# The first pair of each diffusion step: attention groups and scalings put ahead of the looks, and fewer GpSimd operations, in a two-layer graph kernel

## The chip, the cores and the metric

The kernel runs on one core of one Trainium2 chip. The metric is the device time of one execution in microseconds; lower is better. Differences are read in per cent of some 3760 us. The engines are called by the profile's names: PE (TensorE), ACT (ScalarE), DVE (VectorE), POOL (GpSimd), and SP (SyncE), which here only issues DMAs. "PEq", "DVEq" and "SPq" are the engines' instruction queues.

## The reference, cut to what matters

A graph of n = 2708 nodes with 512 features goes through two layers. Layer 0 is graph attention with 8 heads. Layer 1, which the change concerns, is a diffusion in two steps; it has a dense S (the adjacency plus the identity) and an attention that keeps, in each row, the smallest set of largest probabilities whose sum reaches 0.9:

```python
Rf = S / S.sum(axis=1, keepdims=True)
Rb = S / S.sum(axis=0)[:, None]
Xf, Xb, Xa = X, X, X
Z = 0
for s in range(2):
    Q, K = Xa @ W1, Xa @ W3
    logits = Q @ W2 @ K.T
    vals, idx = sorted(logits, descending)          # in each row
    k_i = sum(cumsum(softmax(vals)) < 0.9) + 1
    A = softmax(logits where rank < k_i else -inf)
    Xf, Xb, Xa = Rf @ Xf, Rb @ Xb, A @ Xa
    Z = Z + (Xf @ U1[s] + Xb @ U2[s] + Xa @ U3[s])
Y = X + Z                                           # then layer norm, and the residual
```

The sorted and cumulated part is not done by sorting: the kernel looks for a threshold in each row above which the mass is 0.9.

## The kernel before, in words

**Tiling.** The 2708 rows are 22 tiles of 128 rows (the last has 20). Two tiles are a pair (`grp`, 11 pairs), four tiles a quad. Layer 0 takes until about 1086 us of the profiled span, step 0 of layer 1 until about 2311, step 1 the rest. In layer 1 `S` and the split features lie in HBM and are streamed for each quad; the values `va` and the keys stay in SBUF.

**What is done for a pair**, in `class Logits` (L490) and the functions behind it:

- `queries` (L499) loads the queries `q_t`. `products` (L508) multiplies them with the keys on PE (L517), six chunks for a tile, and ACT copies each chunk from PSUM into the logits tile `p` (L519). The pool of `p` has four buffers, so the products of pair g+2 can be copied only when the search of pair g is done with its tiles. Its end is a branch on DVE (L884).
- `exp` (L522) takes the row maxima on DVE (L544) and returns a list of steps: for each tile `root` (L552 and L549: the exponentials of half the logits, for their sum) and `full` (L556: the exponentials in place, with their sum) on ACT; `points` (L559 to L572: three first guesses of the threshold, small operations on POOL); the looks (L549), two passes of ACT over `p` for each of three points and two tiles, twelve in all; and `masses` (L574 to L577, POOL), which makes of the looks' sums the mass above each guess.
- `search` (L592) runs on DVE: it picks the bracket from the looks (L619 to L641), then makes rounds (two in step 0, four in step 1), each with a pass over `p` for each tile (L624). After its first round it calls `early`, which starts `exp` of the next pair. Then it calls `late` (below) and `finish` (L793). `finish` makes a copy of `p` below the threshold in `keep` (L800), takes its eight largest (L802; in step 1 twice), finds the exact cut, and writes the kept row into `keep` (L722, or L728 where step 1 ranks ties). A switch at L884 goes to rarely used arms: ties (L736), more rounds (MORE_ROUNDS), bisection. `rden` (L901) is the reciprocal of the kept mass.
- `attended` (L996): the kept rows are turned on PE (L1006) in groups of four tiles, copied to `at` by ACT (L1010), and multiplied with `va` (L1025). There are 6 groups for a row tile, 12 for a pair. The scaled sum is `xa` (L1033).
- `part` (L941): the diffusion of a quad, S times the features. One `product` (L949) loads `hl` (L955) and `s_r` (L957) on SP's queue and makes 8 matmuls (L961). At the end of a part its `scaled` steps (L964) scale the rows on ACT (L967) into the tile `xe` of a pool with two buffers, store that on POOL's queue to `xfb_d` (L968), and in step 0 split it for the next step (`split_rows`, L175: L181 and L182 on DVE, a store on POOL's queue at L183, two buffers).
- `diffused` (L986) loads the scaled rows of a pair back as `x0`, `x1` (L991, SP). `mixed` (L1040) turns them and `xa` on PE (L147) and multiplies them with the three `U` (L1056 loads, L1058).

**The order of the work.** On PE, ACT, DVE and SP the program's order is the order of execution (`manual_schedule`); POOL's order is the planner's. Each pass of the main loop (index g, L1165 on) overlaps three pairs: the logits of pair g+2, the search of pair g+1 and the attention of pair g. Work is put between the matmuls of attention from two lists: `fills` (the steps of `exp`, mostly for ACT) and `others` (products, scalings, loads of the diffusion); `paced(list, n)` runs the next n of a list. The lists `looks` and `left` exist only for the first pairs: the pass g = -1 has no attention, so it leaves six looks and the masses, and the scalings of the part that it worked on (eight in step 0, four in step 1), to the pass g = 0. Before the change that pass puts lg[2]'s products first, then all left looks, then search and attention, with the left scalings and the loads of `diffused` at the head of `others`.

Of the kernel before, what the change touches and what calls it, by code (L numbers as in the profile page):

```python
# [9 lines left out]
F32 = mybir.dt.float32  # L10
# [5 lines left out]
OP = mybir.AluOpType  # L16
# [8 lines left out]
P = 128  # L25
# [6 lines left out]
X_LO = math.exp(-4.0)  # L32
# [5 lines left out]
ABOUT = (0.88, 1.0, 1.12)  # L38
# [15 lines left out]
def kernel(  # L54
# [415 lines left out]
    for s in range(STEPS):  # L470
        for i in range(2):
            nc.vector.memset(powers[:, s, i], GUESS[s][i])
    weights = const.tile([P, G + 1], F32, name="weights")
# [14 lines left out]
    class Logits:  # L488
# [33 lines left out]
        def exp(self, looks=True):  # L522
# [5 lines left out]
            self.tot = small.tile([P, G], F32, name="tot")  # L528
            self.half = small.tile([P, G], F32, name="half")
# [8 lines left out]
            if self.ragged:  # L538
                for x in (self.tot, self.half, self.above, self.signs, self.pts):
                    nc.gpsimd.memset(x, 1.0)  # L540
# [18 lines left out]
            def points():  # L559
                x0 = small.tile([P, 2, G], F32, name="x0")  # L560
                gp.tensor_tensor(x0[:, 0], self.tot, powers[:, self.s, 0], op=OP.pow)
                gp.tensor_tensor(x0[:, 1], self.half, powers[:, self.s, 1], op=OP.pow)
                gp.tensor_tensor(x0[:, 0], x0[:, 0], x0[:, 1], op=OP.mult)
                gp.tensor_scalar(x0[:, 0], x0[:, 0], math.exp(GUESS[self.s][2]), X_LO * 1.5, op0=OP.mult, op1=OP.max)
                for j, m in enumerate(ABOUT):
                    gp.tensor_scalar(self.pts[:, j, 0], x0[:, 0], m, 0.9995, op0=OP.mult, op1=OP.min)
                gp.tensor_tensor(self.th, self.pts[:, :, 0], self.pts[:, :, 0], op=OP.mult)
                gp.tensor_tensor(self.th, self.th, self.th, op=OP.mult)
                gp.tensor_scalar(self.nth, self.th, -1.0, None, op0=OP.mult)  # L569
                gp.tensor_scalar(self.thr, self.tot, P_NUC, None, op0=OP.mult)  # L570
                gp.tensor_scalar(self.top, self.tot, 1.0 + CURVE, None, op0=OP.mult)
                gp.tensor_scalar(self.cap, self.tot, CAP, None, op0=OP.mult)  # L572
# [10 lines left out]
            if looks:  # L583
                for i, t in enumerate(self.grp):
# [8 lines left out]
    def search(lg, looked, early, late):  # L593
# [199 lines left out]
        def finish(go):  # L793


            for i, pr in tiles:
                t, m = th[:pr, i:i + 1], kept[:pr, 1, i:i + 1]
                for e in range(0, nx, 8):
                    vs, ss = vn[:pr, i, e:e + 8], sn[:pr, i, e:e + 8]
                    v.scalar_tensor_tensor(keep[i][:pr], ps_[i][:pr], t, ps_[i][:pr], op0=OP.is_lt, op1=OP.mult,  # L800
                                           accum_out=left[:pr, i:i + 1] if e else None)
                    v.max(vs, keep[i][:pr])  # L802
# [105 lines left out]
    for s in range(STEPS):  # L908
        last = s == STEPS - 1
        with ExitStack() as st:  # L910
# [26 lines left out]
            def part(half, b):  # L937
# [26 lines left out]
                def scaled(t, ps, i, inv, to):  # L964
                    pr = rows[t]
                    x = work.tile([P, D], F32, name="xe")
# [14 lines left out]
            def paced(steps, n):  # L981
                for step in steps[:n]:
                    step()
                del steps[:n]
# [10 lines left out]
            def attended(grp, keep, rden, fills, others, then):  # L995
# [21 lines left out]
                for n, (i, t, cs) in enumerate(steps):  # L1017
# [18 lines left out]
                    at = nxt  # L1036
                return xa, at

# [107 lines left out]
            with tc.manual_schedule(engines={PE, ACT, DVE, SP}):  # L1146
# [18 lines left out]
                for g in range(-1, NP):  # L1165

                    fills = []
                    if g + 2 < NP:
                        lg[g + 2].products()
                    paced(looks, len(looks))  # L1170
# [7 lines left out]
                    if g >= 0:  # L1178
                        left.append(lambda g=g: rows_in.extend(diffused(pairs[g])))
                    others = left + part(half, g + 2)  # L1180
                    left = []
# [6 lines left out]
                    def late(g=g):  # L1188
                        if g >= 0:
                            keep, rden = ready  # L1190
                            if g:
                                paced(others, 1)
                            final = g == NP - 1 and not last
                            xa, v_t = attended(pairs[g], keep, rden, fills, others,
                                               lambda: None if final else turned_rows(pairs[g], rows_in[0]))
# [53 lines left out]
```

## Time and profile before

| | |
|---|---|
| median of three runs | 3761.26 us (3754.86, 3761.26, 3762.85) |
| the profiled execution | 3750.71 us |
| its span on the core | 3748.9 us |
| mean granted TensorE clock | 0.959 |
| layer 0; step 0; step 1 (from the timeline) | to 1086; to 2311; to 3749 us |

The profiled execution is one of its own, beside the three runs; the span is the part of it from the first to the last instruction. The tables of the profile are for that one execution.

A timeline line reads: start in us, duration in us, engine, line of the kernel, operation, output and inputs with sizes, how many instructions are taken together, and in brackets the idle time of the engine just ahead, with what ended it. A line of waits reads: engine and what it wanted to run, the releaser, total us, times, and the longest. The clock in stretches says how fast PE was allowed to run:

```
stretch of the span        PEclk
1196 to 1327 us (pair 0, step 0)   0.86
1430 to 2311 us (rest of step 0)   0.98
2490 to 2633 us (pair 0, step 1)   0.88
2633 to 3640 us (rest of step 1)   0.99
```

### The profile page before, as it was taken

The numbers are of one execution on the slowest core, as the hardware profiler recorded it, in microseconds if no ns is written. First come the engines' busy times: TensorE is split into PE (matmuls) and PEld (weight loads), VectorE is DVE, ScalarE is ACT, GpSimd is POOL, SyncE is SP. The second block draws the span as 40 slices with busy tenths as digits, with TensorE's granted clock in tenths as the row PEclk, the third lists the DMA queues.
The fourth block names the chain that finished last, engine by engine and source line by source line (L and its number), as shares of the span: only waits on it lengthen the run. The fifth ranks groups of instructions, "written<-read, shape, count | busy, mean of one in ns | idle before, by whom it ended". The sixth has DMA issues, their size and how long they took to land. (4 is left out here: it accounts for less than half of the span.)

```text
span 3748.9 us, 35397 instructions
## 1 busy us (share of the span) xinstructions
PE 3377.5 (90%) x11143; PEld 1759.3 (47%) x11143; DVE 2612.2 (70%) x4814; ACT 1540.2 (41%) x2334; POOL 836.7 (22%) x1187
## 2 busy tenths in 40 slices
PE   8999999999855898989899899668999999999888
PEld 4433333333433455545455453435555665556442
DVE  4588898989946536474454652966879788777991
ACT  2344202111026565555666622334644556445511
POOL 4115151423331121121212120302222111111101
PEclk9999999999977899999999999889999999999999
DMA  3476424233144555454545353836556765567552
GB/s 116 155 258 224 155 80 136 89 101 109 50 147 163 190 185 178 154 178 147 196 148 207 108 189 119 300 101 234 194 192 210 252 207 188 192 210 240 191 200 72
DMA packets 276459, 634.09 MB, mean 169 GB/s; under 512 B 37209, under 2 KB 70441, under 8 KB 273243
## 3 DMA queue, kind: packets, MB, share of 16 engines
q1 hardware_dynamic: 249183, 540.99, 43.4%
q0 software_dynamic: 27024, 90.30, 6.4%
q8 instruction: 89, 1.46, 0.2%
q14 instruction: 163, 1.34, 0.1%
HBM read 509.07 MB, written 122.10 MB: 168 GB/s over the span
## 5 line engine op out<-in xcount | busy, mean ns | idle before, releaser
L1025 PE MATMUL a<-va,at 128*128 128x512 f32 (+2 forms) x1936 | 898.0, 603 | 57.9 <-ACT at L1010 57.7
L961 PE MATMUL q<-hl,s_r 128*128 128x512 f32 x2904 | 823.3, 430 | 69.1 <-DMA s_r<-s_d 67.6
L429 PE MATMUL po<-e,fw 128*65 128x512 f32 (+4 forms) x2112 | 836.7, 551 | 31.1 <-DVE e L427 22.6
L427 DVE SCALAR_TENSOR_TENSOR e<-r_b,kk,a_c 128x512 f32<-128x512 f32 (+4 forms) x1056 | 750.9, 740 | 64.9 <-PE po L429 13.8
L961 PEld LDWEIGHTS q<-hl,s_r 128*128 128x128 f32 x2904 | 547.9, 191 | 313.5 <-issue 158.9
L549 ACT ACTIVATE junk_a<-p,nth 128x2708 uint8<-128x2708 f32 (+1 forms) x240 | 613.1, 2554 | 93.4 <-POOL nth L569 89.8
L1025 PEld LDWEIGHTS a<-va,at 128*128 128x128 f32 (+2 forms) x1936 | 339.9, 188 | 428.5 <-issue 347.2
L429 PEld LDWEIGHTS po<-e,fw 128*65 128x65 f32 (+1 forms) x2112 | 285.3, 139 | 542.9 <-issue 267.4
L1058 PE MATMUL a<-u_k,v_t 128*128 128x512 f32 (+1 forms) x1056 | 490.2, 601 | 22.0 <-ACT xa L1033 14.7
L624 DVE SCALAR_TENSOR_TENSOR junk<-p,th 128x2708 bf16<-128x2708 f32 (+1 forms) x132 | 402.3, 3048 | 4.0
L1010 ACT COPY at<-t 128x512 f32<-128x512 f32 (+3 forms) x308 | 140.2, 476 | 440.3 <-PE t L1006 439.7
L1058 PEld LDWEIGHTS a<-u_k,v_t 128*128 128x128 f32 (+1 forms) x1056 | 188.8, 186 | 240.0 <-issue 185.6
L517 PE MATMUL t<-keys,q_t 128*128 128x452 f32 x528 | 167.8, 445 | 108.6 <-ACT p L519 87.9
L800 DVE SCALAR_TENSOR_TENSOR keep<-p,th 128x2708 f32<-128x2708 f32 (+1 forms) x44 | 133.4, 3033 | 132.2 <-PE t L1006 131.0
L181 DVE TENSOR_SCALAR split_hl<-xe 128x512 int32<-128x512 int32 (+1 forms) x44 | 19.0, 433 | 272.9 <-ACT xe L967 232.5
L802 DVE MAX8 vn<-keep 128x8 f32<-128x2708 f32 (+1 forms) x66 | 196.8, 2982 | 2.3
L519 ACT COPY p<-t 128x452 f32<-128x452 f32 (+2 forms) x264 | 132.3, 539 | 147.4 <-DVEq L884 74.8
L411 ACT ACTIVATE s_c<-a_c 128x512 fp32r<-128x512 f32 (+3 forms) x132 | 76.2, 578 | 247.1 <-DMA a_c<-in_adj_t_dram 121.8
L517 PEld LDWEIGHTS t<-keys,q_t 128*128 128x128 f32 x528 | 92.0, 211 | 179.9 <-ACT p L519 141.4
L1006 PE MATMUL t<-ident,keep 128*128 128x128 f32 (+1 forms) x968 | 147.4, 274 | 24.4 <-DVE keep L752 16.7
L1006 PEld LDWEIGHTS t<-ident,keep 128*128 128x128 f32 (+1 forms) x968 | 115.1, 139 | 107.6 <-issue 80.4
L544 DVE TENSOR_REDUCE nmx<-p 128x1 f32<-128x2708 f32 (+1 forms) x44 | 129.2, 2967 | 36.1 <-ACT p L519 35.8
(294 smaller groups left out, 3099.1 us busy)
## 6 DMA issues: line engine op xcount, KB each, us to landing
s_r<-s_d SPq DMA_DIRECT2D x330, 256.0 KB
hl<-vhl_d SPq DMA_DIRECT2D x132, 512.0 KB
u_k<-in_L_gnn_U_dram SPq DMA_DIRECT2D x264, 256.0 KB
hl<-fhl_d SPq DMA_DIRECT2D x132, 512.0 KB
hl<-bhl_d SPq DMA_DIRECT2D x132, 512.0 KB
arow<-in_adj_dram SPq DMA_DIRECT2D x21, 1354.0 KB
s_d<-s_c SPq DMA_DIRECT2D x88, 256.0 KB
a_c<-in_adj_t_dram SPq DMA_DIRECT2D x84, 256.0 KB
```

The source lines that it names most:

```text
L427: nc.vector.scalar_tensor_tensor(e[:pr, :cw], r_b[:pr, i, :cw], kk[:pr, t, hd:hd + 1], a_c[t][:pr, :cw], op0=OP.max, op1=OP.mult)
L429: nc.tensor.matmul(po[i][:, :cw], lhsT=fw[:pr, t, hd, :], rhs=e[:pr, :cw], start=(t == 0), stop=(t == NT - 1))
L517: nc.tensor.matmul(pl[:, :c1 - c0], lhsT=q[:, i], rhs=self.keys[:, c0:c1], start=(i == 0), stop=(i == 1))
L549: nc.scalar.activation(junk[:pr], self.p[i][:pr], func, **kw)
L624: v.scalar_tensor_tensor(junk_b[:pr], ps_[i][:pr], th, ps_[i][:pr], op0=OP.is_ge, op1=OP.mult, accum_out=dst)
L800: v.scalar_tensor_tensor(keep[i][:pr], ps_[i][:pr], t, ps_[i][:pr], op0=OP.is_lt, op1=OP.mult, accum_out=left[:pr, i:i + 1] if e else None)
L802: v.max(vs, keep[i][:pr])
L961: nc.tensor.matmul(half[j], lhsT=s_r[:, j * P:(j + 1) * P], rhs=hl[:, h], start=(c == 0 and h == 0), stop=(c == NT - 1 and h == 1))
L1006: nc.tensor.transpose(pt[:rows[c], j, :pr], keep[i][:pr, cols[c]], ident[:pr, :pr])
L1010: nc.scalar.copy(at[:r, j0:j1, :pr], pt[:r, j0:j1, :pr])
L1025: nc.tensor.matmul(pa[:pr], lhsT=at[:rows[c], j, :pr], rhs=va[:rows[c], c, :], start=(c == 0), stop=(c == NT - 1))
L1058: nc.tensor.matmul(pz[i][:rows[t]], lhsT=v_t[i][:, k, :rows[t]], rhs=u_k, start=(n == 0 and k == 0), stop=(n == 2 and k == KD - 1))
```

## The change

Eight edits, all in layer 1:

1. In the first pass with attention (g = 0) the left scalings go ahead. In step 1 all four come ahead of lg[2]'s products; in step 0 four come ahead of them and four behind them, ahead of attention. Before, they were paced between the attention groups.
2. In step 1, four products of the next part go ahead of lg[2]'s products in that pass.
3. `attended` becomes a generator that stops after each group, and in that pass it is advanced one group for every two of the left looks. Before, all left looks came ahead of attention.
4. The loads of `diffused` go, in that pass, behind the first third of `others`; in the other passes they go to its head, as before.
5. `points` makes 10 GpSimd operations for 13: one power over the two sums, one product with the three factors, one clamp. The factors are a constant tile, filled once by six DVE memsets.
6. An empty step stands between `points` and the looks, so each look comes one place later in `fills`.
7. `finish` writes the passes below the threshold of both tiles into keep[0].
8. `xe` has four buffers in step 0; in step 1, for the first two parts, the odd tiles use a tile `xw` with two buffers of its own.

The number of instructions is the same on PE, ACT and SP; on DVE there are six more. The diff, cut to its core:

```diff
--- before.py
+++ after.py
@@ -470,6 +470,10 @@
     for s in range(STEPS):
         for i in range(2):
             nc.vector.memset(powers[:, s, i], GUESS[s][i])
+    about = const.tile([P, STEPS, len(ABOUT), G], F32, name="about")
+    for s in range(STEPS):
+        for j, m in enumerate(ABOUT):
+            nc.vector.memset(about[:, s, j], m * math.exp(GUESS[s][2]))
     weights = const.tile([P, G + 1], F32, name="weights")
     for i in range(G + 1):
         nc.vector.memset(weights[:, i:i + 1], float(1 << i))
@@ -525,8 +529,8 @@
             _, small, _ = self.pools
             gp = nc.gpsimd
             grp = self.grp
-            self.tot = small.tile([P, G], F32, name="tot")
-            self.half = small.tile([P, G], F32, name="half")
+            self.sums = small.tile([P, 2, G], F32, name="sums")
+            self.tot, self.half = self.sums[:, 0], self.sums[:, 1]
             self.pts = small.tile([P, NA, 3, G], F32, name="pts")
             self.th = small.tile([P, NA, G], F32, name="th_a")
@@ -536,7 +540,7 @@
             self.signs = small.tile([P, NA, G], F32, name="signs", bufs=1)
             self.ragged = any(rows[t] < P for t in grp) or len(grp) < G
             if self.ragged:
-                for x in (self.tot, self.half, self.above, self.signs, self.pts):
+                for x in (self.sums, self.above, self.signs, self.pts):
                     nc.gpsimd.memset(x, 1.0)
             nmx = small.tile([P, 2, G], F32, name="nmx1")
             for i, t in enumerate(self.grp):
@@ -558,13 +562,12 @@
             def points():
                 x0 = small.tile([P, 2, G], F32, name="x0")
-                gp.tensor_tensor(x0[:, 0], self.tot, powers[:, self.s, 0], op=OP.pow)
-                gp.tensor_tensor(x0[:, 1], self.half, powers[:, self.s, 1], op=OP.pow)
+                gp.tensor_tensor(x0, self.sums, powers[:, self.s], op=OP.pow)
                 gp.tensor_tensor(x0[:, 0], x0[:, 0], x0[:, 1], op=OP.mult)
-                gp.tensor_scalar(x0[:, 0], x0[:, 0], math.exp(GUESS[self.s][2]), X_LO * 1.5, op0=OP.mult, op1=OP.max)
-                for j, m in enumerate(ABOUT):
-                    gp.tensor_scalar(self.pts[:, j, 0], x0[:, 0], m, 0.9995, op0=OP.mult, op1=OP.min)
-                gp.tensor_tensor(self.th, self.pts[:, :, 0], self.pts[:, :, 0], op=OP.mult)
+                x = self.pts[:, :, 0]
+                gp.tensor_tensor(x, x0[:, 0].unsqueeze(1).to_broadcast([P, NA, G]), about[:, self.s], op=OP.mult)
+                gp.tensor_scalar(x, x, X_LO * 1.2, 0.9995, op0=OP.max, op1=OP.min)
+                gp.tensor_tensor(self.th, x, x, op=OP.mult)
                 gp.tensor_tensor(self.th, self.th, self.th, op=OP.mult)
                 gp.tensor_scalar(self.nth, self.th, -1.0, None, op0=OP.mult)
                 gp.tensor_scalar(self.thr, self.tot, P_NUC, None, op0=OP.mult)
@@ -581,6 +584,8 @@
                 steps += [lambda a=(i, rows[t]): root(*a), lambda a=(i, rows[t]): full(*a)]
             steps.append(points)
             if looks:
+                steps.append(lambda: None)
                 for i, t in enumerate(self.grp):
                     for j in range(NA):
                         for func, to in ((AF.Relu, self.above), (AF.Sign, self.signs)):
@@ -793,13 +798,14 @@
         def finish(go):
             for i, pr in tiles:
                 t, m = th[:pr, i:i + 1], kept[:pr, 1, i:i + 1]
                 for e in range(0, nx, 8):
                     vs, ss = vn[:pr, i, e:e + 8], sn[:pr, i, e:e + 8]
-                    v.scalar_tensor_tensor(keep[i][:pr], ps_[i][:pr], t, ps_[i][:pr], op0=OP.is_lt, op1=OP.mult,
+                    v.scalar_tensor_tensor(keep[0][:pr], ps_[i][:pr], t, ps_[i][:pr], op0=OP.is_lt, op1=OP.mult,
                                            accum_out=left[:pr, i:i + 1] if e else None)
-                    v.max(vs, keep[i][:pr])
+                    v.max(vs, keep[0][:pr])
                     if e:
                         m = left[:pr, i:i + 1]
                         v.tensor_tensor(m, tot[:pr, i:i + 1], m, op=OP.subtract)
@@ -963,7 +969,11 @@
                 def scaled(t, ps, i, inv, to):
                     pr = rows[t]
-                    x = work.tile([P, D], F32, name="xe")
+                    if last and b < 2 and t % 2:
+                        x = work.tile([P, D], F32, name="xw", bufs=2)
+                    else:
+                        x = work.tile([P, D], F32, name="xe", bufs=2 if last else 4)
                     nc.scalar.activation(x[:pr], ps[:pr], AF.Copy, scale=inv[:pr, t:t + 1])
                     nc.gpsimd.dma_start(out=xfb_d[i, cols[t], :], in_=x[:pr])
                     if not last:
@@ -1034,7 +1044,15 @@
                         if not last:
                             nc.gpsimd.dma_start(out=xa_d[cols[t], :], in_=xa[i][:pr])
                     at = nxt
+                    yield
                 return xa, at
+            def rest_of(work_):
+                while True:
+                    try:
+                        next(work_)
+                    except StopIteration as done_:
+                        return done_.value
             def turned_rows(grp, v):
                 return [transposed(up, ps_t, v[i], rows[t], "v_t") for i, t in enumerate(grp)]
@@ -1165,9 +1183,15 @@
                 for g in range(-1, NP):
                     fills = []
+                    held = len(left)
+                    paced(left, held if last else held // 2)
+                    others = left + part(half, g + 2)
+                    left = []
+                    if g == 0 and last:
+                        paced(others, 4)
                     if g + 2 < NP:
                         lg[g + 2].products()
-                    paced(looks, len(looks))
                     if g + 3 < NP:
                         lg.append(Logits(pools, s, pairs[g + 3], keys, rank))
                         lg[g + 3].queries()
@@ -1176,9 +1200,16 @@
                     rows_in = []
                     if g >= 0:
-                        left.append(lambda g=g: rows_in.extend(diffused(pairs[g])))
-                    others = left + part(half, g + 2)
-                    left = []
+                        others.insert(0 if g else len(others) // 3, lambda g=g: rows_in.extend(diffused(pairs[g])))
+                        final = g == NP - 1 and not last
+                        att = attended(pairs[g], *ready, fills, others,
+                                       lambda: None if final else turned_rows(pairs[g], rows_in[0]))
+                    if g == 0:
+                        paced(others, held - held // 2 if not last else 0)
+                        while looks:
+                            next(att)
+                            paced(looks, 2)
                     def early(g=g):
                         if g + 2 < NP:
@@ -1187,12 +1218,9 @@
                     def late(g=g):
                         if g >= 0:
-                            keep, rden = ready
                             if g:
                                 paced(others, 1)
-                            final = g == NP - 1 and not last
-                            xa, v_t = attended(pairs[g], keep, rden, fills, others,
-                                               lambda: None if final else turned_rows(pairs[g], rows_in[0]))
+                            xa, v_t = rest_of(att)
                             done.extend(mixed(pairs[g], v_t, *rows_in, xa, others, fills, final))
                             paced(others, len(others))
                             paced(fills, len(fills))
```

## The prediction, on record ahead of the run

> **What bounds the kernel now.** The page first: PE is busy 90% of the span, DVE 70%, so time can only come from stretches where PE stands still. The span in slices shows PE at 5 to 6 tenths where each step of layer 1 starts. The waits of PE then say on what (columns: engine, line, releaser, total us, times, longest).
>
> ```profile
> PE 3377.5 (90%) x11143; PEld 1759.3 (47%) x11143; DVE 2612.2 (70%) x4814; ACT 1540.2 (41%) x2334; POOL 836.7 (22%) x1187
> ...
> PE t L517 <- ACT p L519: 87.9, 79, 11.9
> PE q L961 <- DMA s_r<-s_d: 67.6, 39, 17.5
> PE a L1025 <- ACT at L1010: 57.7, 23, 15.7
> ```
>
> PE's timeline places them. A pair of step 1 takes 116.6 us once steady, with 1.45 us of wait at L517; the long waits lie in pair 0 of each step, the place of the change. Step 0 (its pair 1 begins at 1326.52):
>
> ```profile
> 1187.24 7.72 PE L517 MATMUL t<-keys,q_t 128*128 128x452 f32 x20 [10.51 <-ACT p L519]
> 1211.98 5.59 PE L1025 MATMUL a<-va,at 128*128 128x512 f32 x8 [15.74 <-ACT at L1010]
> 1217.85 3.60 PE L1025 MATMUL a<-va,at 128*128 128x512 f32 x8
> 1241.30 6.29 PE L1025 MATMUL a<-va,at 128*128 128x512 f32 x8 [11.89 <-ACT at L1010]
> 1254.14 6.69 PE L1025 MATMUL a<-va,at 128*128 128x512 f32 x8 [3.62 <-ACT at L1010]
> ```
>
> Step 1 (pair 1 begins at 2632.65):
>
> ```profile
> 2481.46 4.91 PE L517 MATMUL t<-keys,q_t 128*128 128x452 f32 x12 [11.94 <-ACT p L519]
> ...
> 2506.00 5.41 PE L1025 MATMUL a<-va,at 128*128 128x512 f32 x8 [15.74 <-ACT at L1010]
> ...
> 2554.46 3.38 PE L961 MATMUL q<-hl,s_r 128*128 128x512 f32 x8 [17.53 <-DMA s_r<-s_d]
> ```
>
> The 15.74 is six looks (L549, 2.55 + 0.19 us each with the accumulator read) on ACT's queue ahead of the first copy of `at`. The 11.89 and 17.53 come from the scaling; ACT's, DVE's and SP's queues, in that order:
>
> ```profile
> 1240.09 0.69 ACT L967 ACTIVATE xe<-q,rinv 128x512 f32<-128x512 f32 x1 [17.53 <-DVE split_hl L182]
> 2546.06 0.69 ACT L967 ACTIVATE xe<-q,cinv 128x512 f32<-128x512 f32 x1 [10.79 <-DMA xfb_d<-xe]
> 1212.35 0.17 DVE L641 TENSOR_TENSOR pts<-top,pts 128x6 f32<-128x6 f32 x1 [21.11 <-POOL pts L577]
> 1223.29 5.85 DVE L544 TENSOR_REDUCE nmx<-p 128x1 f32<-128x2708 f32 x2
> 2518.23 5.84 DVE L544 TENSOR_REDUCE nmx<-p 128x1 f32<-128x2708 f32 x2
> 2545.99 3.73 SPq L991 DMA_DIRECT2D x<-xfb_d  x2
> 2549.81 0.38 SPq L955 DMA_DIRECT2D hl<-fhl_d  x1
> ```
>
> In step 0 the third scaling waits for a buffer whose split (L181, L182) stands on DVE behind the whole first round of search(1); the copy of `at` behind it lets PE starve. In step 1 the last scaling waits for a DMA of `xe`; the loads of x (L991) wait for that on SP, and hl and s_r of the products wait behind them.
>
> **What the Trainium skill says.** Its page "Perfetto Trace Analysis", Per-engine timelines: ACT, DVE and GpSimd are strictly in order; the trace agrees, an `at` copy whose transposes end at 1229.4 is made only after the 17.53 wait. "TensorE: Matmul & The Clock Gate", Part 1: an idle window of about 3.4 us halves the clock; the trace agrees, the group after 15.74 us of wait takes 5.4 to 5.6 us against 3.60. "SBUF — State Buffer", Who interferes with whom: a DVE instruction with two SBUF inputs and a GpSimd instruction that reads SBUF exclude each other; here POOL's small operations take 2.9 to 3.0 us beside DVE's 3.04 us passes, 0.22 to 0.28 alone.
>
> **Step 0, part by part.** (a) The left scalings (eight) move: four ahead of lg[2]'s products, four behind, all ahead of attention, with four `xe` buffers for two. Each is 0.69 us on ACT. The first four lie in ACT's wait for DVE's branch, which ends at 1186.7 (cost nothing; if the cover is gone, 2.8). The other four cost 4 x 0.69 = 2.8 on ACT from about 1195.4 to 1198.2. Their splits, 8 x 1.1 us, and DMAs (POOL's queue, ahead of the masses) now sit on DVE right after rden at 1190; two split buffers cycle in 3.4 to 4.4 us, so they are done near 1206, before DVE is wanted. (b) One `at` copy goes ahead of each two looks (8 steps in four groups: 7 looks and the masses, since the empty step shifts one look here). First group at 1198.6 instead of 1211.98: the 15.74 wait becomes about 2.5. The four groups run at ACT's pace, 2 x 2.7 + 0.5 = 5.9 us each, as PE needs only 3.9 + 2.1 for a group with one product. (c) Price: seven looks, four scalings and four copies ahead of the masses, end of looks at about 1220, so L641 starts near 1221.3, 9 later than 1212.35. The x loads stand on SP after a third of the products; their rows were written near 1206, so SP has nothing to wait for: 0, and 2 to 4 if it had. Round 0 and the maxima follow as before: first maximum after 1226.2 + 9 = 1235.2; root and full (2 x 2.7) then stand ahead of an `at` copy, at 1241.4. By then PE has run groups 0 to 5 (four at 5.9, two more at 3.9 to 5.9, ending near 1229.7), so it idles again, some 11.7 us before group 6. (d) But group 6 of `at` begins at 1241.4 instead of 1254.14, and five products are done where none were. Of before, 1326.52 − 1254.14 = 72.4; less the cold start (6.69 − 3.60) and the waits 1.52 and 1.29 that the scalings made: 66.5. New end: 1241.4 + 66.5 − 5 x 2.05 = 1297.7, 28.8 earlier. With the products spent, the mixing waits for xa and u_k as pair 1 shows (2.3 to 4.5): I take **25**, range 15 to 30. search(1)'s branch, DVE-side, comes about 19 us ahead of that.
>
> **Step 1.** (e) All four scalings go ahead of everything, with `xw` as second pair of buffers: the 6.13 us of wait at the second of them and the product waits around it shrink, some 6.5 us at 2394.42. It is not a gain: the wait at 2481.46 ends with DVE's branch of search(0). DVE itself waited 1.25 (L624) and 1.38 (L544) in this stretch: 2.6 earlier. (f) Four products (4 x 2.07 = 8.3 us) go ahead of lg[2]'s products, into that 11.94 us wait: 8.3 off later work; if the cover is gone they cost what they save. (g) Looks interleaved as in (b): first group about 2487 instead of 2506.00, looks end near 2508.5, L641 at 2509.6 (+3.2). First root at 2524.4, group 6 at 2527.9 against 2529.45: the 15.74 is here almost wholly turned into a wait of group 6 for DVE's maximum. (h) x's loads stand after a third of the products instead of ahead of all, and the scalings lie a stage back: the 17.53 goes. What is late next is search(1): its `is_lt` pass L800 no longer waits 12.40 for keep[1] (keep[0] for both tiles), branch at about 2602. (i) New end: 2529.45 to 2632.65 is 103.2; less 17.53 and 8.27 it is 77.4; 2527.9 + 77.4 = 2605.3, 27.3 earlier, DVE 3 us ahead. I take **26**, range 18 to 30 (DVE 8 us later would be paid).
>
> **All other pairs.** (j) `points`: 13 GpSimd operations become 10, with 6 memsets on DVE at the start (small, under 1 us, beside layer 0). Three operations save 0.7 us alone, up to 9 blocked; ACT's wait for nth (89.8 us, 19 times) has PE with groups in hand in steady pairs: 0 taken, bounds −1 to +1 per pair. (k) The empty step puts each look one fill slot later: 0 taken, bounds ±1 us for each of 20 pairs, as a look (2.7) may stand ahead of a v_t copy that PE awaits. (l) keep[0] lets DVE start 8 to 12 us earlier in pairs where PE sets the pace: 0. In step 0, four odd-even boundaries wait 7.9 to 8.5 at L517 for DVE's branch, and DVE there waits on splits: four `xe` buffers could save up to 1.4 each, 0 taken as the two split buffers remain.
>
> **Sum.** −25 − 26 = −51; I say −50. Against the profiled execution, 3750.71 (span 3748.9 and 1.8 around it): 3700.7. The median of the runs lies 10.5 above the profiled one: **3711**.
>
> **Rivals.** A, one gain is handed back: the looks end later, so the search, which step 1's pair 1 needs with 3 us to spare, becomes the bound; or the waits only move to group 6. For: DVE's wait of 21 us at L641 is already the looks' fault. Against: in step 0 DVE has 19 us. One step's gain: 3761 − 25 = 3736. B, no change: the later looks of (k) delay the copies of v_t by up to 2.68 us in 18 to 20 pairs, 50 us, all eaten: 3760. Against: steady PE waits are 1.45 us a pair, so slack exists. C, slower: the points' rounding (a power over both sums, a product with `about`, floor X_LO*1.2 for X_LO*1.5) lets a search miss its bracket, so that it takes the arm with MORE_ROUNDS and a second finish. In step 1 a three-round stretch to the branch took 47 us (2433.7 to 2480.8); with the rounds it is some 74, less 10 to 15 of slack: 60 a case. From the first such case on it loses 10: 3771. Against: the same formula in fp32, changed only in its last bits. That the edit doesn't do what it says is partly in (g).
>
> **Numbers.** Both gains: 0.62, at 3711, own range 3695 to 3726. A: 0.24, 3736. Larger gain (blocked GpSimd time given back, a warmer clock): 0.06, down to 3685. B: 0.04. C: 0.04. The range 3688 to 3745 leaves out B, C and a part of the larger gain. A measurement here tells about 0.2% (7.5 us) from no change: faster 0.92, same 0.04, slower 0.04.
>
> **What would show it.** PE's timeline after: no 15.74 before the first group of attention in either step; in step 0 a wait of 10 to 12 before group 6, released by ACT's copy behind the maxima; pair 1 of step 0 beginning near 1298, that of step 1 29 + 25 earlier than 2632.65 in all, without the 17.53. L641 9 us later in step 0, 3 in step 1. Steady pairs of step 1 at 116.6. Wrong, if those pairs lengthen by a us or more, if pair 1's first L517 waits for DVE's branch, or if products or u_k wait for loads put on SP in another order.

## The result, and the profile after

| | before | after |
|---|---|---|
| median, us | 3760.87 (four runs, 3754.86 to 3762.85) | 3712.36 (four runs, 3710.75 to 3715.51) |
| the profiled execution, us | 3750.71 | 3711.47 |
| its span, us | 3748.9 | 3709.7 |

The ratio after to before is 0.9875, 95% interval 0.9858 to 0.9892: the changed kernel is 1.25% faster. The medians differ by 48.5 us, where 50 were forecast. (The median of before has one run more here than in the table ahead of the prediction.)

PE's busy time fell by only 1.4 us (3377.5 to 3376.1), so nearly all of the gain is idle time of PE. The page's line of engines and the waits of PE, after (L521 is L517 of before, L523 is L519, L967 is L961, L1035 is L1025, L1020 is L1010):

```profile
PE 3376.1 (91%) x11143; PEld 1757.7 (47%) x11143; DVE 2612.0 (70%) x4820; ACT 1541.7 (42%) x2334; POOL 808.4 (22%) x1119
```

```profile
PE t L521 <- ACT p L523: 73.6, 80, 12.9
PE q L967 <- DMA s_r<-s_d: 60.9, 39, 15.6
PE a L1035 <- ACT at L1020: 39.5, 23, 15.0
```

The three sums fell by 14.3, 6.7 and 18.2 us, 39.2 in all, as much as the two spans differ. The timeline of PE after, pair 0 of step 0 and then of step 1 (the last line of each is the start of pair 1):

```profile
1205.38 5.23 PE L1035 MATMUL a<-va,at 128*128 128x512 f32 x8 [5.19 <-ACT at L1020]
...
1248.36 5.92 PE L1035 MATMUL a<-va,at 128*128 128x512 f32 x8 [10.29 <-ACT at L1020]
...
1307.69 1.46 PE L521 MATMUL t<-keys,q_t 128*128 128x452 f32 x4
```

```profile
2458.45 6.76 PE L967 MATMUL q<-hl,s_r 128*128 128x512 f32 x16 [3.46 <-DMA s_r<-s_d]
...
2474.12 3.70 PE L1035 MATMUL a<-va,at 128*128 128x512 f32 x8 [0.24 <-ACT at L1020]
...
2513.36 6.59 PE L1035 MATMUL a<-va,at 128*128 128x512 f32 x8 [15.03 <-ACT at L1020]
...
2593.21 1.38 PE L521 MATMUL t<-keys,q_t 128*128 128x452 f32 x4
```

The waits of 15.74 us ahead of the first group are 5.19 and 0.24; the 17.53 for the loads of step 1 is gone. In both steps a wait stands before group 6, the first of the pair's second row tile. DVE's timeline says for what: it takes the masses later, and the maxima (L548, L544 of before) come behind round 0, which comes behind the masses.

```profile
1228.34 0.17 DVE L646 TENSOR_TENSOR pts<-top,pts 128x6 f32<-128x6 f32 x1 [11.98 <-POOL pts L580]
1239.28 5.84 DVE L548 TENSOR_REDUCE nmx<-p 128x1 f32<-128x2708 f32 x2
...
2495.08 0.17 DVE L646 TENSOR_TENSOR pts<-top,pts 128x6 f32<-128x6 f32 x1 [27.78 <-POOL pts L580]
2506.95 5.85 DVE L548 TENSOR_REDUCE nmx<-p 128x1 f32<-128x2708 f32 x2
```

**Which lengths to compare.** Layer 0, whose matmuls and order are the same in all kernels, ends early in the profiled execution of before: step 0's first logits matmul starts at 1090.46 there, at 1095.30 after, and at 1094.2 to 1101.0 in the eleven profiles of the experiments. So the places of two profiles are not compared, but lengths inside each: in step 0 from `rden` of the first search, and also from the step's first logits matmul, to the start of pair 1; in step 1 from the first logits matmul of pair 1 (in the pass g = -1) to the start of pair 2, so that a wait at the head of pair 1 counts.

| kernel | step 0 from `rden`, us | step 0 from its first matmul, us | step 1, us | median, us |
|---|---|---|---|---|
| before | 136.6 | 236.1 | 362.7 | 3760.87 |
| after | 110.8 | 212.4 | 340.1 | 3712.36 |
| small_edits | 134.8 | 234.2 | 365.9 | 3758.76 |
| step0_only | 110.9 | 212.8 | 365.3 | 3736.43 |
| step1_only | 135.7 | 234.5 | 333.8 | 3729.55 |
| looks_block | 116.7 | 219.0 | 339.0 | 3718.66 |
| scalings_back | 121.1 | 219.9 | 366.8 | 3744.98 |
| two_buffers | 123.7 | 222.5 | 343.2 | 3724.10 |
| no_products_ahead | 112.7 | 213.9 | 353.0 | 3725.79 |
| max_early | 100.1 | 201.9 | 331.4 | 3690.00 |
| looks_sooner | 116.7 | 216.9 | 320.4 | 3692.77 |
| sooner_and_max | 103.8 | 203.6 | 320.8 | 3684.42 |
| max_and_sooner_in_step1 | 100.7 | 200.7 | 318.2 | 3676.98 |

Step 0 gained 25.8 us from `rden`, but only 23.7 from its first matmul, because `rden` itself came later after the change. ACT's first copy of the logits is released by DVE's branch (at 1186.66 before, 1190.87 after), and `rden` is the first thing that DVE does behind the branch:

```profile
1189.90 0.17 DVE L901 RECIPROCAL rden<-den 128x2 f32<-128x2 f32 x1 [4.91 <-issue]
...
1196.93 0.17 DVE L907 RECIPROCAL rden<-den 128x2 f32<-128x2 f32 x1 [7.72 <-issue]
```

DVE stood still for 4.91 us ahead of `rden` before and for 7.72 after. In the four other kernels without the early scalings in step 0, or with only two buffers for them, it was 4.90 to 5.11; in all eight with both it was 5.94 to 7.90. The profile names no cause ("issue"), and it stays open. So step 0 is counted from its first matmul below. Step 1 gained 22.6, which makes 46.3 together for a difference of medians of 48.5. Over all kernels, such sums miss the difference of the medians to after by up to 4.5 us. The experiments were timed in three rounds, each beside its own runs of before, whose medians are 3758.28, 3761.14 and 3760.92; a difference between kernels of different rounds carries that spread.

### The profile page after: what moved, and what is told of

Read it like the earlier page. It is cut to its first block, busy times and chain, and to the rows that moved or that the text cites. A ratio compares the mean times of both kernels' runs of the same rounds, so it can differ in the third digit from the quotient of the medians.

```text
span 3709.7 us, 35331 instructions
## 1 busy us (share of the span) xinstructions
PE 3376.1 (91%) x11143; PEld 1757.7 (47%) x11143; DVE 2612.0 (70%) x4820; ACT 1541.7 (42%) x2334; POOL 808.4 (22%) x1119
## 5 line engine op out<-in xcount | busy, mean ns | idle before, releaser
L1035 PE MATMUL a<-va,at 128*128 128x512 f32 (+2 forms) x1936 | 895.6, 602 | 39.6 <-ACT at L1020 39.5
L967 PE MATMUL q<-hl,s_r 128*128 128x512 f32 x2904 | 824.5, 430 | 61.1 <-DMA s_r<-s_d 60.9
L967 PEld LDWEIGHTS q<-hl,s_r 128*128 128x128 f32 x2904 | 547.9, 191 | 306.3 <-issue 135.4
L1035 PEld LDWEIGHTS a<-va,at 128*128 128x128 f32 (+2 forms) x1936 | 339.2, 188 | 408.5 <-issue 346.7
L1076 PE MATMUL a<-u_k,v_t 128*128 128x512 f32 (+1 forms) x1056 | 491.4, 603 | 19.6 <-ACT xa L1043 14.4
L1020 ACT COPY at<-t 128x512 f32<-128x512 f32 (+3 forms) x308 | 140.4, 477 | 478.6 <-PE t L1016 478.4
L521 PE MATMUL t<-keys,q_t 128*128 128x452 f32 x528 | 165.3, 439 | 94.7 <-ACT p L523 73.6
L523 ACT COPY p<-t 128x452 f32<-128x452 f32 (+2 forms) x264 | 132.2, 539 | 123.2 <-PE t L521 85.6
L521 PEld LDWEIGHTS t<-keys,q_t 128*128 128x128 f32 x528 | 90.1, 208 | 165.4 <-ACT p L523 126.4
L548 DVE TENSOR_REDUCE nmx<-p 128x1 f32<-128x2708 f32 (+1 forms) x44 | 129.1, 2966 | 43.4 <-ACT p L523 43.4
L565 POOL TENSOR_TENSOR x<-sums,powers 128x4 f32<-128x4 f32 x22 | 43.7, 1987 | 507.9 <-ACT p L560 481.9
```

Of the source, the lines that this page charges most:

```text
L521: nc.tensor.matmul(pl[:, :c1 - c0], lhsT=q[:, i], rhs=self.keys[:, c0:c1], start=(i == 0), stop=(i == 1))
L523: nc.scalar.copy(p[:pr, c0:c1], pl[:pr, :c1 - c0])
L967: nc.tensor.matmul(half[j], lhsT=s_r[:, j * P:(j + 1) * P], rhs=hl[:, h], start=(c == 0 and h == 0), stop=(c == NT - 1 and h == 1))
L1020: nc.scalar.copy(at[:r, j0:j1, :pr], pt[:r, j0:j1, :pr])
L1035: nc.tensor.matmul(pa[:pr], lhsT=at[:rows[c], j, :pr], rhs=va[:rows[c], c, :], start=(c == 0), stop=(c == NT - 1))
L1076: nc.tensor.matmul(pz[i][:rows[t]], lhsT=v_t[i][:, k, :rows[t]], rhs=u_k, start=(n == 0 and k == 0), stop=(n == 2 and k == KD - 1))
```

## The experiments

The theory was that of the prediction: two separate gains in the first pairs, nothing elsewhere. Open was which edit earned them: the looks between the groups, the early scalings, or the buffers.

### Nothing elsewhere: edits 5 to 7 alone (small_edits)

The kernel before, with

```diff
+                gp.tensor_tensor(x0, self.sums, powers[:, self.s], op=OP.pow)
...
+                steps.append(lambda: None)
...
-                    v.scalar_tensor_tensor(keep[i][:pr], ps_[i][:pr], t, ps_[i][:pr], op0=OP.is_lt, op1=OP.mult,
+                    v.scalar_tensor_tensor(keep[0][:pr], ps_[i][:pr], t, ps_[i][:pr], op0=OP.is_lt, op1=OP.mult,
```

and the rest of `points` and the constant `about` as in the change.

> The kernel before with edits 5 to 7 alone (points in 10 operations, the empty step, keep[0]). Theory (they cost and save nothing on the path): ratio to before 0.999 to 1.001, pairs 1 to 10 of step 1 still 116.6 us apart. One thing moves in pair 0: the empty step leaves seven looks and not six to be made ahead of attention, so up to 2.7 us later in each step, +5 in all. Rival (the later looks delay copies, 1 to 2.7 us a pair): +20 to +50 us. Rival (GpSimd time was on the path): -10 to -20 us.

Measured: 3758.76 against 3758.28 us, ratio 1.0003, interval 0.9994 to 1.0012. Pairs of step 1 stay 116.6 apart; the first pair of step 1 lost 3.2 us (of the 5 expected in all from the one look more; step 0 lost nothing). So rivals B (the empty step) and C (the points' rounding) of the prediction fall. The GpSimd operations and the empty step were changed together: a small saving of the one under a small cost of the other is not excluded, but it lies within that interval. keep[0] did let DVE end its search some 10 us sooner in the odd pairs of step 0 (rden at 1518.87 for 1529.41), where nothing waits for it.

### The two steps apart (step0_only, step1_only)

```diff
-        last = s == STEPS - 1
+        last = s == STEPS - 1
+        new = s == 0                     # step1_only: new = last
...
-                        while looks:
+                    if g == 0 and new:
...
+                    if not new:
+                        paced(looks, len(looks))
```

> The kernel after with pair 0 of step 1 arranged as before (scalings paced between attention groups with two buffers, looks ahead of attention, no products ahead, loads of x behind the scalings). Theory: only step 0's gain is left, 25.9 us by the pair's start in the two profiles, so a ratio of about 0.993. Rival (most of the gain lies in step 1, or the two depend on each other): 0.997 or nearer to 1.

> The kernel after with pair 0 of step 0 arranged as before. Theory: only step 1's gain is left, 22.1 us by the two profiles, ratio about 0.994; the two single gains add up to the whole 48. Rival: 0.997 or nearer to 1, the sum short of the whole.

Measured: ratios 0.9936 (0.9919 to 0.9952) and 0.9917 (0.9901 to 0.9934), 21.9 and 28.7 us below before (3758.28), 50.6 together for the whole's 48.5: two gains, each within its forecast range (15 to 30, 18 to 30), that add up. In step1_only the same step 1 took 333.8 us where after took 340.1. The difference lies ahead of attention, in the stretch of products from the pass g = -1 to lg[2]'s first matmul: 91.5 us there, 96.4 in after, with PE stopped many times for `s_r`. The same stretch, in the same order, took 95.3 us in looks_block and 96.6 in max_early. Whether step1_only's 91.5 is chance or belongs to that kernel is not shown, so one profile of step 1 is read here no better than to some 5 us.

### The looks between the groups (looks_block)

```diff
-                        while looks:
-                            next(att)
-                            paced(looks, 2)
+                        paced(looks, len(looks))
```

> The kernel after with edit 3 alone undone: the seven left looks are all made ahead of attention. Theory (interleaving only exchanges the wait before the first group for the one before group 6, which is for the maxima behind the first round): in step 1 group 6 starts at the same time, some 47 us behind rden, so it loses 0 to 3 us; in step 0, where five products use the groups' gaps, it loses 4 to 8 us; the whole is 5 to 10 us above after, ratio to before about 0.989 to 0.9905. Rival (the two 15.74 us waits were worth their length): 25 to 30 us above after, ratio about 0.995.

Measured: 3718.66, ratio 0.9890 (0.9874 to 0.9907), 6.3 us above after: step 0 lost 6.6, step 1 nothing (-1.1). The two intervals overlap (after's is 0.9858 to 0.9892), though none of the four runs of either kernel lies among the other's; 6.3 is small and known only roughly. PE's timeline of looks_block:

```profile
1223.46 5.29 PE L1035 MATMUL a<-va,at 128*128 128x512 f32 x8 [23.39 <-ACT at L1020]
...
2498.29 6.16 PE L1035 MATMUL a<-va,at 128*128 128x512 f32 x8 [18.41 <-ACT at L1020]
```

The first groups wait 23.39 and 18.41 us, but no group 6 waits after that. So the change's most visible part exchanges one wait for another of nearly the same length. It pays in step 0 alone, where products fill the gaps between the groups.

### The place of the scalings (scalings_back)

```diff
-                    paced(left, held if last else held // 2)
-                        paced(others, 4)
+                        paced(others, 0)
-                        others.insert(0 if g else len(others) // 3,
+                        others.insert(0 if g else held,
-                        paced(others, held - held // 2 if not last else 0)
```

> The kernel after with edits 1, 2 and 4 undone (the left scalings and the loads of x are paced between the attention groups again, no products ahead), looks still interleaved, the four buffers kept. Theory (most of the gain is the scalings' place: products that fill gaps, and loads that do not wait for a store): pair 1 of step 0 begins 8 to 15 us later than in after, that of step 1 15 to 25 us later; ratio to before about 0.994 to 0.998. Rival (the buffers alone took the 17.53 waits away): less than 8 us above after in all, ratio 0.9895 or less.

Measured: 3744.98, ratio 0.9958 (0.9942 to 0.9975), 32.6 us above after: step 0 lost 7.5 and step 1 26.7, more than it had gained. PE's and SP's timelines of scalings_back in step 1:

```profile
2545.72 3.75 PE L967 MATMUL q<-hl,s_r 128*128 128x512 f32 x8 [19.31 <-DMA s_r<-s_d]
2538.14 1.31 SPq L1001 DMA_DIRECT2D x<-xfb_d  x2
```

The wait of 17.53 us is back although ACT no longer waits for a buffer there: its four scalings run from 2526.24 to 2529.1 and the loads of x, which read what the scalings' stores write, go out only at 2538.14, with `hl` and `s_r` behind them on SP. The buffers alone do not help step 1; the place of the scalings and of these loads does. The run undid edits 1, 2 and 4 together, so their shares are not separated, except that of edit 2 (below).

Why are the stores so late? They stand on POOL's queue behind `points` of the next pair. So they did before the change. POOL's timeline of before shows two of these operations, which take some 3 us each while DVE makes its passes, and the first store, which is issued behind the last but one:

```profile
2534.97 2.89 POOL L570 TENSOR_SCALAR thr<-tot 128x2 f32<-128x2 f32 x1
2537.92 3.00 POOL L571 TENSOR_SCALAR top<-tot 128x2 f32<-128x2 f32 x1
2543.57 0.65 POOL L968 DMA_DIRECT2D xfb_d<-xe  x1 [0.26 <-issue]
```

In before, ACT had begun these scalings at 2534.01, so 9.6 us passed until the first store was issued; in scalings_back it was 9.4 (2526.24 to 2535.68), with two operations of 3.04 and 3.00 us. That is about half of the length of PE's waits of 17.53 and 19.31 us; by how much they would shrink with POOL free was not tested. After the change the first store goes out at 2450.59, 1.0 us behind the start of its scaling, with no `points` in front of it.

### The buffers (two_buffers)

```diff
-                    if last and b < 2 and t % 2:
+                    if False:
-                        x = work.tile([P, D], F32, name="xe", bufs=2 if last else 4)
+                        x = work.tile([P, D], F32, name="xe", bufs=2)
```

> The kernel after with edit 8 undone: two xe buffers in both steps, no xw. The third scaling of step 0 then waits for the first's split, which stands on DVE behind rden, and ACT's copies of lg[2]'s logits stand behind that scaling. Theory (the early place of the scalings rests on the buffers): in step 0 the copies start 5 to 12 us later, so pair 1 begins 5 to 12 us later; in step 1 the scalings wait 2 to 4 us for stores, 0 to 3 us later; ratio to before 0.989 to 0.9915. Rival (the buffers do nothing, the place does it all): within 2 us of after.

Measured: 3724.10, ratio 0.9903 (0.9886 to 0.9919), 11.7 us above after; step 0 lost 10.1, step 1 3.1. ACT's timeline of two_buffers:

```profile
1196.46 0.69 ACT L977 ACTIVATE xe<-q,rinv 128x512 f32<-128x512 f32 x1 [10.97 <-DVE split_hl L182]
1197.43 0.69 ACT L977 ACTIVATE xe<-q,cinv 128x512 f32<-128x512 f32 x1 [0.29 <-DVE split_hl L182]
1198.02 0.96 ACT L523 COPY p<-t 128x452 f32<-128x452 f32 x2
```

The third scaling waits for the first split, which DVE makes after rden, and the copies of the logits stand behind it. In step 0 the early place without the buffers (222.5 us) is no better than the late place with them (219.9, scalings_back); the late place with two buffers and interleaved looks was not run.

### The four products (no_products_ahead)

```diff
-                        paced(others, 4)
+                        paced(others, 0)
```

> The kernel after with edit 2 undone: no products of the next part ahead of lg[2]'s products in step 1. In after PE came to those products some 3 to 6 us behind DVE's branch, because the four products ahead waited for their loads. Theory (the cover of the four products was only partly there): attention starts 3 to 6 us earlier, 8.3 us of products come later, so pair 1 of step 1 begins 2 to 5 us later than in after, ratio to before about 0.988 to 0.989. Rival (the wait covered all of it): 8 us later, 0.9897.

Measured: 3725.79, ratio 0.9903 (0.9887 to 0.9920), 13.4 us above after, more than theory and rival gave. Pair 1 began only some 3 us later than in after by the length from the first logits matmul (227.4 for 224.6), as the theory had it, but then lost 10 more at its head. ACT's and PE's timelines of no_products_ahead:

```profile
2608.20 0.69 ACT L977 ACTIVATE xe<-q,rinv 128x512 f32<-128x512 f32 x1 [6.54 <-DMA xfb_d<-xe]
2608.79 0.97 ACT L523 COPY p<-t 128x452 f32<-128x452 f32 x2
```

```profile
2609.37 6.71 PE L521 MATMUL t<-keys,q_t 128*128 128x452 f32 x16 [8.68 <-ACT p L523]
```

Four products more in pair 0 push the next part's scalings to the pair's very end (from 2596.81 on), and the last of them waits for a store of its buffer, ahead of the copies for pair 1. So edit 2 is worth some 3 us by itself, its 8.3 us less what its loads cost, and those 10.

### What PE waits for before group 6 (max_early)

The kernel after, with the maxima of pair 2 taken ahead of the wait for the masses:

```diff
+        def maxima(self):
+            self.nmx = self.pools[1].tile([P, 2, G], F32, name="nmx1")
+            for i, t in enumerate(self.grp):
+                pr = rows[t]
+                nc.vector.tensor_reduce(self.nmx[:pr, 0, i:i + 1], self.p[i][:pr], axis=AX.X, op=OP.max, negate=True)
...
+                        lg[g + 2].maxima()
                         while looks:
```

> The kernel after with one move more: in the pass g = 0 the maxima of pair 2 (5.85 us on DVE) stand ahead of the wait for the masses of pair 1, where DVE is idle 12 us in step 0 and 28 us in step 1, and not behind the first round. Theory (PE's waits of 10.3 and 15.0 us before group 6 are for these maxima): both waits fall by 8 us or more, pair 1 of step 0 begins 8 to 12 us earlier, that of step 1 3 to 13 us earlier (then DVE's branch of search(1) may end last), in all 12 to 22 us faster than after. Rival (the waits before group 6 are for something else on ACT, such as the points of a search, or the search ends last at once): less than 4 us.

Measured: 3690.00, ratio 0.9818 (0.9802 to 0.9835), 22.4 us below after. PE's timeline of max_early, group 6 of each step and the head of pair 1 of step 1, with ACT's line for the latter:

```profile
1240.41 3.60 PE L1041 MATMUL a<-va,at 128*128 128x512 f32 x8
...
2485.82 3.60 PE L1041 MATMUL a<-va,at 128*128 128x512 f32 x8
...
2572.21 7.85 PE L522 MATMUL t<-keys,q_t 128*128 128x452 f32 x20 [8.14 <-ACT p L524]
2571.62 0.97 ACT L524 COPY p<-t 128x452 f32<-128x452 f32 x2 [7.75 <-DVEq L896]
```

Both waits are gone, and group 6 runs in 3.60 us for 5.92 and 6.59. That the waits were for the maxima is shown. In step 1, DVE's search then ends last: ACT waits for its branch, and PE 8.14 us for ACT.

### Looks in an earlier idle stretch (looks_sooner, sooner_and_max, max_and_sooner_in_step1)

ACT's timeline of after, in the pass g = -1 and at its end in step 1, asks a question that neither kernel answers:

```profile
2449.60 0.69 ACT L977 ACTIVATE xe<-q,cinv 128x512 f32<-128x512 f32 x1 [33.15 <-PE q L967]
...
2465.66 0.97 ACT L523 COPY p<-t 128x452 f32<-128x452 f32 x2 [13.63 <-PE t L521]
```

Behind its fifth look ACT stood still for 33.15 us, and then 13.63; seven looks at 2.74 us are 19.2.

```diff
-                        paced(fills, 5 + G * NA)
+                        paced(fills, len(fills) if last else 7 + G * NA)
```

> The kernel after with more looks made in the pass g = -1: in step 1 all of them and the masses, in step 0 two more. There ACT is idle 31 and 14 us (step 1) and 5 us (step 0) behind its last look. Theory (those places are free; the looks between the groups hold the start of search(1)): search(1) of step 1 starts 15 to 25 us earlier and ends well ahead of PE, group 6 no longer waits 15 us; step 1's pair 1 begins 12 to 18 us earlier, step 0's 3 to 6 us earlier: 15 to 24 us below after. Rival (search(1)'s end then waits for PE's turns of keep, or the products of the pass g = -1 slow down): 0 to 6 us.

> The kernel after with both the looks of looks_sooner and the early maxima of max_early. Theory: max_early left a wait of 8.14 us at pair 1 of step 1 for DVE's branch and groups at ACT's pace (5.7 us for 3.9); both go, so it is 8 to 14 us below max_early (3690.0), about 3676 to 3682. Rival (the two moves remove the same wait): within 3 us of the better of the two.

Measured: looks_sooner 3692.77, ratio 0.9821 (0.9804 to 0.9837), 19.6 us below after. Step 1 gained 19.7 and step 0 lost 4.5: the expectation of a gain there was wrong. (The two make 15.2; this is where the lengths miss the medians most.) sooner_and_max: 3684.42, ratio 0.9794 (0.9778 to 0.9810), 5.6 below max_early, or 8.4 when each is taken from the before of its own round, for 8 to 14 expected: step 1 gained 10.6 and step 0 gave 1.7 back. Its first group in step 0 waits longer. The two looks more put the first four scalings some 5 us later, counted from the step's first matmul. The copies of the logits lose little by that (they start 1.76 us behind DVE's last instruction ahead of the branch, 1.65 in max_early), but the last two of the scalings behind the copies wait 5.00 and 1.65 us for buffers, where it was 1.52 and 0.74 in max_early, and the copies of `at` stand behind them:

```profile
1213.24 5.08 PE L1041 MATMUL a<-va,at 128*128 128x512 f32 x8 [9.00 <-ACT at L1026]
```

In max_early that wait was 4.63. So the last kernel leaves step 0 alone:

```diff
-                        paced(fills, 5 + G * NA)
+                        paced(fills, len(fills) if last else 5 + G * NA)
```

> The kernel after with the early maxima in both steps, and all looks in the pass g = -1 in step 1 only. In step 0 the two looks more ahead of the scalings moved the first group 4 us later in the runs before (its wait rose from 4.63 to 9.00 us). Theory: step 0 as in max_early, step 1 as in sooner_and_max, 2 to 5 us below the latter's 3684.4, ratio to before 0.978 to 0.979. Rival (step 0's difference was chance): the same as sooner_and_max within 1.5 us.

Measured: 3676.98 (3675.40 to 3679.27), ratio 0.9776 (0.9760 to 0.9792), 35 us below after and 7 below sooner_and_max, more than the 2 to 5 expected. Step 0 gave 2.9 of it; step 1, whose code is the same in both, 2.6, so a part is spread. It is faster than both kernels of this case. PE's timeline of it, group 6 and the head of pair 1 in step 1:

```profile
2484.05 3.60 PE L1041 MATMUL a<-va,at 128*128 128x512 f32 x8
...
2562.59 1.11 PE L522 MATMUL t<-keys,q_t 128*128 128x452 f32 x4 [0.30 <-ACT p L524]
```

## Why the prediction was right

- **Step 0, -25:** 23.7 from its first matmul, 25.8 from `rden`. Behind `rden`, (b) the first group was put 8.7 us and came 8.45; (d) group 6 at 51.5 and came at 51.43; (c) L641 at 31.4 and came at 31.41. That this fits so closely is partly luck. Behind ACT's first copy of the logits, the first group was put 11.9 us and came 14.5, group 6 at 54.7 and came at 57.5: `rden` and ACT's queue were late by nearly the same. Two more terms were wrong inside a right sum. The 3.8 us set aside for waits for xa and u_k did not come as waits. In their place was a cold start, that is, a group that runs slower behind a wait, which the sum had struck out: group 6 at 5.92 us for 3.60. The Trainium skill, "TensorE: Matmul & The Clock Gate", What's actually happening, has the clock halved after an idle window; a wait of 11.7 us was in the forecast (10.29 came), and its cold group should have been priced with it. The trace agrees: PE's granted clock was 0.62 in the stretch of that group, and 1.00 in max_early, which has no wait there and the group at 3.60.
- **(a), the scalings and the splits:** the four scalings behind the copies were priced at 2.8 us on ACT. They took 5.5 (1199.38 to 1204.85), because the last two waited for a buffer. The splits, which free the buffers, stand behind `rden`:

```profile
1202.74 0.69 ACT L977 ACTIVATE xe<-q,rinv 128x512 f32<-128x512 f32 x1 [2.09 <-issue]
1204.16 0.69 ACT L977 ACTIVATE xe<-q,cinv 128x512 f32<-128x512 f32 x1 [0.74 <-DVE split_hl L182]
```

The profile names the split for the second wait only; the first ends 0.1 us behind the end of the third split. The splits were taken as done near 1206 and lasted to 1215.3 (18 us behind `rden` instead of 16), four of them waiting 1.7 to 2.5 us for a store. The masses came at 1228.3, so DVE lost nothing by that.
- **Step 1, -26:** 22.6 by the length, and 28.7 by step1_only's time. (g) Group 6 was put 46.4 us behind `rden` and came at 47.4, and cold: 6.59 for 3.60 at a granted clock of 0.55, not priced. (h) The 17.53 wait went, as forecast, though the prediction named only the DMA of `xe` and not `points` on POOL ahead of it. DVE was put 3 us ahead of PE at pair 1. It was some 5 ahead, by an estimate: its last instruction ahead of the branch ended at 2586.35, PE began pair 1 at 2593.21, and where ACT waited for this branch (before, max_early) it was released 1.4 us behind that instruction. max_early, which moves PE up, meets the branch.
- **(e), 2.6 us of slack on DVE:** 0.8. From the first logits matmul of pair 1 to rden of search(0) it took 98.2 us before and 97.3 after.
- **(f), the cover of the four products:** mis-sized both ways. It did not hold: ACT waited for PE's products (13.63 <-PE t L521), and two of the four had to wait 3.46 us for their loads. But the edit is worth 13.4 us by the medians and not 8.3, since without it the next part's scalings end up on the boundary to pair 1. The prediction counted a moved step's own time and not what its absence does to the end of the list.
- **(j) to (l), nothing elsewhere:** small_edits shows 1.0003 for the three together.
- **Rival A** (one gain handed back) did not come about, though its half, that the waits only move to group 6, was a fact: it made the looks' new place worth 6.3 us of 48.5.

What the sum hid was which edit bore it. Undone one at a time, the scalings and what goes with them cost 32.6, the products among them 13.4, the buffers 11.7, the looks 6.3; these overlap and are not to be added. The two profiles' spans differ by 39.2 where the medians differ by 48.5: 4.8 us of this is layer 0, 2.2 the stretch of step 0 ahead of `rden`, the rest lies in small pieces. Why the execution of before had a layer 0 shorter than all others is left open. So the 10.5 us that the prediction added to get from a profiled execution to a median belonged to that one execution: after's profiled execution came at 3711.47 and not 3700.7, 0.9 below its median. The forecast of the median was not hurt, since the gain was in effect taken from before's median.

## What to carry to other kernels

When a wait is removed by moving work of an in-order engine, follow the chain to the next thing that this work delays, and price the new wait with its cold start: here seven looks between groups won 6 us of the 31 that the two old waits showed. Look for idle time of the same engine ahead of the old place before splitting the work up behind it: 33 us of it stood open a stage earlier, and a reduction that needs nothing of the wait belongs in front of it. A load that waits for a store holds every load behind it on its queue, so the step that makes the store wants to be a stage ahead, with buffers that let it and with no other work in front of the store on its own queue.

## What the runs showed of the hardware

- In pair 0 of both steps, over all profiles, waits of 3.4 to 23.4 us ahead of an attention group were followed by eight matmuls in 5.1 to 6.7 us, waits of 1.1 to 2.4 us by eight in 3.70, and 3.60 was the time without a wait. So each of the longer waits cost 1.5 to 3.1 us more than its length. The shortest of the longer ones (3.4 to 5.3 us) all ended within 15 us of another long wait.
- The same stretch of products fed by DMA (the rest of the pass g = -1 and four more), in the same order, took 91.5 to 96.6 us in four executions (step1_only, looks_block, after, max_early).
- With three operations fewer in `points` for each pair, POOL's busy time was 28 us less in the profile (836.7 to 808.4), and the kernel's time did not change measurably (small_edits).
- DVE stood idle ahead of its first instruction behind the branch of step 0's first search for 4.9 to 5.1 us in five kernels and 5.9 to 7.9 in the eight that make four scalings early, with four buffers; the profile names no cause.
- In before, two GpSimd operations on 128x2 elements took 2.89 and 3.00 us beside DVE's passes of 3.04 us, and the next, with no pass beside it, 0.22 (2534.97, 2537.92 and 2540.98).
